# Mixing tokens by constant matrices with Strassen's seven products, on a TensorE-bound kernel

## The chip, the cores and the metric

The kernel runs on one core of a Trainium2 chip. The metric is the device time of one execution, in microseconds (us). A profile of one execution goes with each kernel. Engines in it are PE (TensorE matmul), PEld (TensorE weight load), DVE (VectorE), ACT (ScalarE), POOL (GpSimd) and SP (SyncE, which issues the DMAs). A line number such as L292 is a line of the kernel that was profiled, so the same instruction has another number in another kernel.

## The reference, cut to what matters

There are 32 batches of 512 tokens with 128 features, and one constant 512x512 matrix `adj`. Four layers follow each other, each as `x = x + layer(relu(layernorm(x)))`:

```python
# layer 0: att is a masked softmax made of adj, M the identity
out = einsum('ij,bjg->big', att * M, h @ W[0]) + einsum('ij,bjg->big', att * (1 - M), h @ W[1]) + bias
# layer 1: Chebyshev hops of adj, given twice
x1 = einsum('bnf,nw->bwf', h, A);  x2 = 2 * einsum('bnf,nw->bwf', x1, A) - h
out = relu(concat(h, x1, x2, x1, x2) @ Theta1 + bias)
# layer 2: message passing with adj squared element by element
messages = einsum('nm,bnd->bmd', adj * adj, relu(h @ psi))
out = relu(concat(messages, h) @ phi1) @ phi2 + phi2_b
# layer 3: attention, exp(8 tanh(. / 8)) * adj, normalised
```

In layers 0, 1 and 2 the tokens are mixed by matrices that are the same for every batch: `att` without its diagonal, `adj` and `cheb = 2 adj adj - I`, and `adj * adj`.

## The kernel before

All is float32. Batches go in pairs (16 pairs). A coroutine for each pair and layer emits the work, and a list scheduler in the compiler sets the order in which each engine gets it. The preparation builds `att` and `cheb`; for pairs 0 to 3 it also does the first part of layer 0 (normalising, transposing, the product `p_g` with W[1]). The mixings are these:

```python
def mixed(h, mat, tag, name, copy):          # layers 1 and 2, one batch
    p = bank(f"p_{name}")                    # a PSUM bank
    for t in range(NT):                      # NT = 4 blocks of 128 tokens
        nc.tensor.matmul(p, h[:, t, :], mat[:, t, :], start=(t == 0), stop=(t == NT - 1))
    s = late.tile([P, N], F32, tag=tag, name=name)
    copy(s, p)
    return s

def layer0(q):                               # one pair, both batches side by side
    hT, g = early.pop(q)
    hd = [straight(hT, b, adiag, f"hd_{q}_{b}") for b in range(2)]     # GpSimd
    ...
    for t0 in range(0, NT, 2):
        po = bank(f"p_l0_{q}_{t0}").rearrange("p (t b f) -> p t b f", t=2, b=2)
        for i in range(2):
            for s in range(NT):
                nc.tensor.matmul(po[:, i], attT[:, s, blk(t0 + i)], g[:, s], start=(s == 0), stop=False)
            for b in range(2):
                nc.tensor.matmul(po[:, i, b], hd[b][:, blk(t0 + i)], w0[:, 0, :], start=False, stop=(b == 1))
        nc.vector.tensor_add(xv, po, xv)
```

From pair 4 on the transposed tile is made by VectorE (32x32 blocks) and two DMAs through DRAM: `hb`, `d`, `hT`. All of x is loaded in the first 25 us.

## Time and profile before

The median was 1062.07 us (3 runs, 1061.74 to 1065.86). A layer is timed here from TensorE's first instruction of it to its first of the next, and layer 3 from its first score product (`p_score`), though a few of its projections already stand among the last products of layer 2. The last layer ends with the span.

| stage | before, us | what TensorE does per pair |
|---|---|---|
| preparation | 67.5 | builds att and cheb |
| layer 0 | 172.7 | mixing, diagonal, p_g: 10.48 us where nothing waits |
| layer 1 | 305.5 | two mixings and three projections: 19.10 us |
| layer 2 | 226.8 | p_feat, one mixing, p_phi, p_l: 13.88 us |
| layer 3 | 288.7 | scores, attention |

The lines behind this table, and how they are read, are in the prediction below: TensorE is busy 97% of the span, and the one large hole is at the start of layer 0.

### The profile page before, as it was taken

To read this page: it belongs to the slowest core of one execution; us is meant where nothing else is said; L and a number is where in the kernel's file an instruction comes from. 1 tells how busy PE (TensorE), PEld (TensorE's weight loads), DVE (VectorE), ACT (ScalarE), POOL (GpSimd) and SP (SyncE) were. 2 spreads that over 40 slices of the span, in tenths; PEclk is the share of its full clock that TensorE was granted. 3 is DMA by queue.
4 is the path that set the end of the run, shared out by engine and by line. 5 is a ranking of instruction groups with operands and counts; after the bars stand their busy time and mean duration, and the time that the engine had idled before them with its cause. 6 is when DMAs were issued, how large, how long until landed. Compare 5 with 4: busy or idle time off the path is not lost.

```text
span 1061.2 us, 13502 instructions
## 1 busy us (share of the span) xinstructions
PE 1025.7 (97%) x4966; PEld 698.4 (66%) x4966; DVE 561.5 (53%) x1280; ACT 413.7 (39%) x877; POOL 233.4 (22%) x214
## 2 busy tenths in 40 slices
PE   4996999999999999999989999999999999999997
PEld 3566999995565665655655555555567777777775
DVE  8924666643243342432655787666675444544443
ACT  5722333501132221322756532222275555544443
POOL 3332444322000000000633200000023333333332
PEclk9998999999999999999999999999999999999999
DMA  9525233421112121121434333222212121121111
GB/s 274 128 55 144 80 88 112 133 66 37 44 49 71 40 64 56 42 78 40 139 80 119 116 102 105 77 78 80 79 51 90 53 68 59 61 65 56 50 31 40
DMA packets 82226, 84.91 MB, mean 80 GB/s; under 512 B 7152, under 2 KB 72944, under 8 KB 82160
## 3 DMA queue, kind: packets, MB, share of 16 engines
q1 hardware_dynamic: 82160, 84.05, 27.4%
q8 instruction: 39, 0.64, 0.3%
q14 instruction: 27, 0.22, 0.1%
HBM read 42.08 MB, written 39.85 MB: 77 GB/s over the span
## 4 chain that ended last, share of the span: by engine, by line
PE 89%; SPq 4%; DMA 2%; ACT 2%; issue 2%; DVE 1%; POOL 0%; POOLq 0%; DVEq 0%; ACTq 0%
PE p_msgT L241 11%; PE p_x1T L241 10%; PE p_x2T L241 10%; PE p_l L257 10%; PE p_av L558 10%; PE p_score L546 10%; PE p_l L470 9%; PE p_feat L257 3%; PE p_hv L257 3%; PE p_phi L516 3%; PE p_phi L517 3%; PE p_qkh L534 2%; PE p_g L257 2%; PE p_l L472 2%; SPq L96 2%; SPq L108 2%
## 5 line engine op out<-in xcount | busy, mean ns | idle before, releaser
L200 ACT ACTIVATE h<-x,sh,rs 128x128 f32<-128x128 f32 x384 | 154.2, 482 | 29.2 <-DVE hb_hT L227 15.4
L551 POOL TENSOR_TENSOR ex<-ex,adjTx 128x512 f32<-128x512 f32 x64 | 83.3, 1303 | 333.1 <-ACT ex L549 324.0
L227 DVE STREAM_TRANSPOSE hb_hT<-h 128x512 f32<-128x512 f32 x120 | 82.7, 699 | 103.3 <-ACT h L200 86.4
L558 PEld LDWEIGHTS p_av<-hv,ex 128*128 128x128 f32 x1024 | 118.7, 191 | 11.6 <-issue 6.9
L558 PE MATMUL p_av<-hv,ex 128*128 128x129 f32 x1024 | 121.3, 275 | 2.3 <-POOL ex L551 2.0
L547 ACT ACTIVATE ex<-p_score 128x512 f32<-128x512 f32 x128 | 71.8, 587 | 130.8 <-PE p_score L546 78.7
L470 PE MATMUL p_l<-g,attT 128*128 128x256 f32 x512 | 122.0, 381 | 0.0
L241 PE MATMUL p_msgT<-sq,feat 128*128 128x512 f32 x256 | 114.0, 598 | 3.2 <-ACT feat L508 3.2
L546 PE MATMUL p_score<-qkh,hT 128*128 128x512 f32 x256 | 115.1, 592 | 0.0
L241 PE MATMUL p_x1T<-adj_s,h 128*128 128x512 f32 x256 | 115.1, 592 | 0.0
L241 PE MATMUL p_x2T<-cheb,h 128*128 128x512 f32 x256 | 115.1, 592 | 0.0
L470 PEld LDWEIGHTS p_l<-g,attT 128*128 128x128 f32 x512 | 93.1, 192 | 10.2
L183 DVE BATCH_NORM_STATS2 bn<-x 128x6 f32<-128x256 f32 x256 | 93.3, 415 | 1.8
L241 PEld LDWEIGHTS p_msgT<-sq,feat 128*128 128x128 f32 x256 | 49.1, 192 | 64.9 <-issue 57.8
L241 PEld LDWEIGHTS p_x2T<-cheb,h 128*128 128x128 f32 x256 | 48.6, 190 | 61.2 <-issue 61.0
L186 ACT ACTIVATE sd<-bn,eps 128x8 f32<-128x8 f32 x64 | 18.0, 299 | 176.9 <-DVE bn L183 176.9
L241 PEld LDWEIGHTS p_x1T<-adj_s,h 128*128 128x128 f32 x256 | 47.4, 190 | 53.6 <-issue 53.3
L551 DVE TENSOR_TENSOR ex<-ex,adjTx 128x512 f32<-128x512 f32 x64 | 45.8, 716 | 65.5 <-ACT ex L549 65.5
L243 ACT COPY x2T<-p_x2T 128x512 f32<-128x512 f32 x32 | 18.7, 584 | 152.8 <-PE p_x2T L241 152.7
L549 ACT ACTIVATE ex<-ex 128x512 f32<-128x512 f32 x128 | 76.5, 630 | 1.8
L546 PEld LDWEIGHTS p_score<-qkh,hT 128*128 128x128 f32 x256 | 46.2, 190 | 46.4 <-issue 44.5
L243 DVE COPY x1T<-p_x1T 128x512 f32<-128x512 f32 x32 | 22.1, 691 | 99.8 <-PE p_x1T L241 99.8
(129 smaller groups left out, 1392.6 us busy)
## 6 DMA issues: line engine op xcount, KB each, us to landing
d_hT<-hb_hT SPq DMA_DIRECT2D x240, 128.0 KB, 2.4
hT<-d_hT SPq DMA_DIRECT2D x60, 512.0 KB, 3.3
x<-in_x_dram SPq DMA_DIRECT2D x32, 256.0 KB, 5.5
out_dram<-x SPq DMA_DIRECT2D x32, 256.0 KB, 2.3
adj_s<-in_adj_dram SPq DMA_DIRECT2D x4, 256.0 KB, 3.4
adjTx<-adjT SPq DMA_DIRECT2D x16, 64.0 KB, 2.0
adjx<-adj_s SPq DMA_DIRECT2D x16, 64.0 KB, 2.0
th<-in_L_gnn_Theta_dram SPq DMA_DIRECT2D x1, 320.0 KB, 5.9
```

The source lines that it names most:

```text
L183: nc.vector.bn_stats(st[:, k].rearrange("p e s -> p (e s)"), xt[q][:, b, t : t + 2, :].rearrange("p t f -> p f t"))
L200: nc.scalar.activation(h[:, b, t, :], xt[q][:, b, t, :], AF.Relu, bias=shift[q][:, i : i + 1], scale=scale[q][:, i : i + 1])
L227: nc.vector.transpose(hb[:, :, b].rearrange("p j t r -> p t j r"), h[:, b].rearrange("p t (j c) -> p t j c", c=QR))
L241: nc.tensor.matmul(p, h[:, t, :], mat[:, t, :], start=(t == 0), stop=(t == NT - 1))
L243: copy(s, p)
L257: nc.tensor.matmul(p[:, blk(t)], hT(t), w, start=(i == 0), stop=(i == len(terms) - 1))
L470: nc.tensor.matmul(po[:, i], attT[:, s, blk(t0 + i)], g[:, s], start=(s == 0), stop=False)
L546: nc.tensor.matmul(ps, hT[:, t, b, :], qkh, start=True, stop=True)
L547: nc.scalar.activation(ex[:, t, :], ps, AF.Tanh, scale=1.0 / (8.0 * math.sqrt(D)))
L549: nc.scalar.activation(ex[:, t, :], ex[:, t, :], AF.Exp, scale=8.0)
L551: eng.tensor_mul(ex[:, t, :], ex[:, t, :], adjTx[:, t, :])
L558: nc.tensor.matmul(po[:, i, : D + 1], ex[:, t, blk(i0 + i)], hv[:, t, :], start=(t == 0), stop=(t == NT - 1))
```

## The change

A product of 2x2 block matrices takes eight block products, or seven by Strassen's scheme in Winograd's form, if some blocks are added before and some results after. Here the matrix is constant, so its block sums are formed once. A pair of batches gives the other factor its 2x2 blocks (two halves of tokens by two batches). The intent is to have an eighth fewer TensorE columns in the mixings of layers 0, 1 and 2, with the additions on engines that have time. Memory for this comes from four square tiles in place of five, and from loading the upper half of x during layer 0.

```diff
+    def sum_blocks(mat, name, eng):          # once for a matrix; a21 is overwritten in place
+        eng.tensor_sub(s3, a11, a21)
+        eng.tensor_add(a21, a21, a22)
+        eng.tensor_sub(s2, a21, a11)
+        eng.tensor_sub(s4, a12, s2)
+        return {1: a11, 2: a12, 3: s4, 4: a22, 5: a21, 6: s2, 7: s3}
+    def right_blocks(half, name, engs):      # for each pair: four subtractions, "rt"
+    ORDER = ((1, "a", True), (6, "c", True), (5, "d", True), (7, "c", False), (2, "a", False),
+             (4, "c", False), (3, "d", False))      # product, bank, first into the bank
     ...
+            if k == 1:   nc.scalar.copy(u[:, 0], pv)                # read out a partial sum,
+            elif k == 6: nc.vector.tensor_add(u[:, 1], pv, u[:, 0]) # then more is added to the bank
     ...
+    sums["att"] = sum_blocks(attT, "att", nc.vector)
+    sums["adj"] = sum_blocks(adj_s, "adj", nc.gpsimd)
+    sums["cheb"] = sum_blocks(cheb, "cheb", nc.gpsimd)
     ...
-            nc.vector.tensor_copy(g[:, :, b, :], pg)
+            (nc.scalar.copy if b else nc.vector.tensor_copy)(g[:, :, b, :], pg)
     ...
+    for q in range(NQ // 2, NQ):
+        waiting[q - NQ // 2].append(loads(q))       # x of pair q, eight pairs ahead
```

Layer 0 uses `right_blocks` with VectorE and GpSimd by turns; layers 1 and 2 use GpSimd alone. `sums["sq"]` for layer 2 is formed by GpSimd during layer 1.

More of the change, by code (lines that the diff above doesn't have):

```diff
@@ L66 @@
     const = ctx.enter_context(tc.tile_pool(name="const", bufs=1))
-    xpool = ctx.enter_context(tc.tile_pool(name="xpool", bufs=NQ))
+    xpool = ctx.enter_context(tc.tile_pool(name="xpool", bufs=NQ // 2))
     stats = ctx.enter_context(tc.tile_pool(name="stats", bufs=NQ + 2))
@@ L83, in square_tile @@
     def square_tile(name):
-        return const.tile([P, NT, N], F32, tag="square", name=name, bufs=5)
+        return const.tile([P, NT, N], F32, tag="square", name=name, bufs=4)
     def crossed(ap):
@@ L103 @@
     xt = []
-    for q in range(NQ):
+    for q in range(NQ // 2):
         xt.append(xpool.tile([P, 2, NT, D], F32, tag="x", name=f"x_{q}"))
@@ L136 @@
     kw = load_rows(k_w, "kw")[:, 0, :]
-    for b in range(8, B):
+    for b in range(8, B // 2):
         load_x(b)
@@ L235, in transposed @@
         return hT
-    def mixed(h, mat, tag, name, copy):
-        p = bank(f"p_{name}")
-        for t in range(NT):
-            nc.tensor.matmul(p, h[:, t, :], mat[:, t, :], start=(t == 0), stop=(t == NT - 1))
-        s = late.tile([P, N], F32, tag=tag, name=name)
-        copy(s, p)
-        return s
+    H = N // 2
+    sums = {}
+    def sum_blocks(mat, name, eng):
+        a11, a12 = mat[:, 0:2, 0:H], mat[:, 2:4, 0:H]
+        a21, a22 = mat[:, 0:2, H:N], mat[:, 2:4, H:N]
+        extra = const.tile([P, 3, 2, H], F32, tag="sums", name=f"sums_{name}", bufs=3)
+        s2, s3, s4 = extra[:, 0], extra[:, 1], extra[:, 2]
+        eng.tensor_sub(s3, a11, a21)
[3 more added lines that the diff above has]
+        return {1: a11, 2: a12, 3: s4, 4: a22, 5: a21, 6: s2, 7: s3}
@@ new lines, in right_blocks @@
+    def right_blocks(half, name, engs):
+        t = late.tile([P, 4, 2, D], F32, tag="rt", name=f"rt_{name}", bufs=2)
+        b11, b12, b21, b22 = half(0, 0), half(0, 1), half(1, 0), half(1, 1)
+        engs[0].tensor_sub(t[:, 0], b12, b11)
+        engs[1].tensor_sub(t[:, 1], b22, t[:, 0])
+        engs[2].tensor_sub(t[:, 2], b22, b12)
+        engs[3].tensor_sub(t[:, 3], b21, t[:, 1])
+        return {1: b11, 2: b21, 3: b22, 4: t[:, 3], 5: t[:, 0], 6: t[:, 1], 7: t[:, 2]}
+    ORDER = ((1, "a", True), (6, "c", True), (5, "d", True), (7, "c", False), (2, "a", False),
+             (4, "c", False), (3, "d", False))
@@ new lines, in products, with by_feature @@
+    def products(name, form, left, right, evict):
+        banks = {}
+        for k, g, first in ORDER:
+            if first:
+                banks[g] = bank(f"p_{name}_{g}")
+            form(banks[g], left[k], right[k], first)
+            evict(k, banks[g])
+            yield
+    def by_feature(p, a, b, first):
+        for k in range(2):
+            nc.tensor.matmul(p[:, :H], b[:, k, :], a[:, k, :], start=(first and k == 0),
+                             stop=(k == 1), skip_group_check=True)
@@ new lines, in by_token, with mixed, evict, evict2 @@
+    def by_token(p, a, b, first):
+        for i in range(2):
+            for k in range(2):
+                nc.tensor.matmul(p[:, i * D : (i + 1) * D], a[:, k, blk(i)], b[:, k, :],
+                                 start=(first and i == 0 and k == 0), stop=(k == 1),
+                                 skip_group_check=True)
+    def mixed(name, left, right, dst):
+        m1 = late.tile([P, 3, H], F32, tag="u", name=f"u_{name}", bufs=2)
+        def evict(k, p):
+            p = p[:, :H]
+            if k == 1:
+                nc.scalar.copy(m1[:, 0], p)
+            elif k == 6:
+                nc.vector.tensor_add(m1[:, 1], p, m1[:, 0])
+            elif k == 7:
+                nc.vector.tensor_add(m1[:, 2], p, m1[:, 0])
+            elif k == 5:
+                return
+            elif k == 2:
+                nc.scalar.copy(dst[:, 0, :H], p)
+            elif k == 4:
+                nc.vector.tensor_add(dst[:, 0, H:], p, m1[:, 0])
+            elif k == 3:
+                nc.vector.tensor_add(dst[:, 1, :H], p, m1[:, 1])
+        def evict2(k, p):
+            evict(k, p)
+            if k == 5:
+                held.append(p)
+            if k == 7:
+                nc.vector.tensor_add(dst[:, 1, H:], held[0][:, :H], m1[:, 2])
+        held = []
+        return products(name, by_feature, left, right, evict2)
@@ L259, in projected, with pair_tile @@
         return tiles(p)
+    def pair_tile(name):
+        return work.tile([P, 2 * N + 2 * NT], F32, tag="pair", name=name, bufs=5)[:, : 2 * N]
     early = {}
@@ L270, in layer0_first @@
         yield
-        g = work.tile([P, NT, 2, D], F32, tag="g", name=f"g_{q}", bufs=4)
+        g = pair_tile(f"g_{q}").rearrange("p (t b f) -> p t b f", t=NT, b=2)
         for b in range(2):
             pg = projected(f"p_g_{q}_{b}", (at(hT, b), w0[:, 1, :]))
-            nc.vector.tensor_copy(g[:, :, b, :], pg)
+            (nc.scalar.copy if b else nc.vector.tensor_copy)(g[:, :, b, :], pg)
         early[q] = hT, g
@@ L282, in transpose_square @@
             nc.scalar.copy(dst[:, j, :], p)
-    adjT = square_tile("adjT")
+    adjT = prep.tile([P, NT, N], F32, name="adjT")
     cheb = square_tile("cheb")
@@ L385 @@
                                 ecol[:, kk : kk + 1], OP.is_equal, OP.mult)
-    att = square_tile("att")
+    att = prep.tile([P, NT, N], F32, name="att")
     diag = prep.tile([P, NT, P], F32, name="diag")
@@ L428 @@
     cross_rows(adjTx, adjT)
-    adjx = square_tile("adjx")
-    cross_rows(adjx, adj_s)
+    sums["adj"] = sum_blocks(adj_s, "adj", nc.gpsimd)
+    sums["cheb"] = sum_blocks(cheb, "cheb", nc.gpsimd)
     th12 = const.tile([P, 2, D], F32, name="th12")
@@ L447 @@
     late = ctx.enter_context(tc.tile_pool(name="late", bufs=4))
+    for q in range(NQ // 2, NQ):
+        xt.append(late.tile([P, 2, NT, D], F32, tag="x", name=f"x_{q}", bufs=NQ // 2))
     def straight(hT, b, scale, name):
-        s = late.tile([P, N], F32, tag="hs", name=name, bufs=3)
+        s = late.tile([P, N], F32, tag="hs", name=name, bufs=2)
         src = hT[:, :, b, :].rearrange("p b (a c) -> p a b c", c=QR)
@@ L459, in straight, with loads @@
         return s
+    def loads(q):
+        load_x(2 * q)
+        load_x(2 * q + 1)
+        yield
     def layer0(q):
@@ L464, in layer0, with x_of, diagonal @@
         nc.gpsimd.tensor_add(xt[q], xt[q], b0[:, None, None, :].to_broadcast([P, 2, NT, D]))
+        right = right_blocks(lambda J, b: g[:, 2 * J : 2 * J + 2, b, :], f"g_{q}",
+                             (nc.vector, nc.gpsimd, nc.vector, nc.gpsimd))
         yield
-        for t0 in range(0, NT, 2):
-            po = bank(f"p_l0_{q}_{t0}").rearrange("p (t b f) -> p t b f", t=2, b=2)
+        def x_of(I, b):
+            return xt[q][:, b, 2 * I : 2 * I + 2, :]
+        def diagonal(p, I, b, first):
@@ L468, in layer0 @@
             for i in range(2):
-                for s in range(NT):
-                    nc.tensor.matmul(po[:, i], attT[:, s, blk(t0 + i)], g[:, s], start=(s == 0), stop=False)
-                for b in range(2):
-                    nc.tensor.matmul(po[:, i, b], hd[b][:, blk(t0 + i)], w0[:, 0, :], start=False,
-                                     stop=(b == 1))
-            xv = xt[q][:, :, t0 : t0 + 2, :].rearrange("p b t f -> p t b f")
-            nc.vector.tensor_add(xv, po, xv)
+                nc.tensor.matmul(p[:, i * D : (i + 1) * D], hd[b][:, blk(2 * I + i)], w0[:, 0, :],
+                                 start=(first and i == 0), stop=True, skip_group_check=True)
@@ new lines, in layer0, with evict @@
+        u = late.tile([P, 3, 2, D], F32, tag="u", name=f"u_l0_{q}", bufs=2)
+        held = {}
+        def evict(k, p):
+            pv = p[:, :H].rearrange("p (i f) -> p i f", i=2)
+            if k == 1:
+                nc.scalar.copy(u[:, 0], pv)
+                nc.gpsimd.tensor_add(x_of(1, 0), x_of(1, 0), u[:, 0])
+            elif k == 6:
+                nc.vector.tensor_add(u[:, 1], pv, u[:, 0])
+                nc.gpsimd.tensor_add(x_of(0, 1), x_of(0, 1), u[:, 1])
+            elif k == 5:
+                held["d"] = pv
+            elif k == 7:
+                nc.vector.tensor_add(u[:, 2], pv, u[:, 0])
+                nc.vector.tensor_add(u[:, 2], held["d"], u[:, 2])
+                nc.gpsimd.tensor_add(x_of(1, 1), x_of(1, 1), u[:, 2])
+            elif k == 2:
+                diagonal(p, 0, 0, False)
+                nc.vector.tensor_add(x_of(0, 0), pv, x_of(0, 0))
+            elif k == 4:
+                diagonal(p, 1, 0, False)
+                nc.vector.tensor_add(x_of(1, 0), pv, x_of(1, 0))
+            elif k == 3:
+                diagonal(p, 0, 1, False)
+                nc.vector.tensor_add(x_of(0, 1), pv, x_of(0, 1))
@@ L476, in layer0 @@
+        for _ in products(f"l0_{q}", by_token, sums["att"], right, evict):
+            pass
+        p = bank(f"p_l0_{q}_e")
+        diagonal(p, 1, 1, True)
+        nc.vector.tensor_add(x_of(1, 1), p[:, :H].rearrange("p (i f) -> p i f", i=2), x_of(1, 1))
         ln_stats(q)
@@ L481, in layer1 @@
         hT = transposed(h, f"hT1_{q}")
+        right = right_blocks(lambda J, b: h[:, b, 2 * J : 2 * J + 2, :], f"h_{q}", [nc.gpsimd] * 4)
         yield
-        x1T, x2T, hs = [], [], []
-        for b in range(2):
-            x1T.append(mixed(h[:, b], adj_s, "mT", f"x1T_{q}_{b}", nc.vector.tensor_copy))
-            x2T.append(mixed(h[:, b], cheb, "x2T", f"x2T_{q}_{b}", nc.scalar.copy))
-            hs.append(straight(hT, b, None, f"hs_{q}_{b}"))
+        x1T = pair_tile(f"x1T_{q}").rearrange("p (b w) -> p b w", b=2)
+        x2T = pair_tile(f"x2T_{q}").rearrange("p (b w) -> p b w", b=2)
+        mixes = (mixed(f"x1T_{q}", sums["adj"], right, x1T), mixed(f"x2T_{q}", sums["cheb"], right, x2T))
+        for _ in zip(*mixes):
+            pass
+        hs = [straight(hT, b, None, f"hs_{q}_{b}") for b in range(2)]
         yield
         for b in range(2):
-            po = projected(f"p_l1_{q}_{b}", (columns(hs[b]), th[:, 0, :]), (columns(x1T[b]), th12[:, 0, :]),
-                           (columns(x2T[b]), th12[:, 1, :]))
-            y = late.tile([P, NT, D], F32, tag="y", name=f"y1_{q}_{b}", bufs=3)
+            po = projected(f"p_l1_{q}_{b}", (columns(hs[b]), th[:, 0, :]), (columns(x1T[:, b]), th12[:, 0, :]),
+                           (columns(x2T[:, b]), th12[:, 1, :]))
+            y = late.tile([P, NT, D], F32, tag="y", name=f"y1_{q}_{b}", bufs=2)
             nc.vector.tensor_add(y, po, spread(b1, NT))
@@ L505, in layer2 @@
             pf = projected(f"p_feat_{q}_{b}", (at(hT, b), psi))
-            feat.append(late.tile([P, NT, D], F32, tag="y", name=f"feat_{q}_{b}", bufs=3))
+            feat.append(late.tile([P, NT, D], F32, tag="y", name=f"feat_{q}_{b}", bufs=2))
             nc.vector.tensor_add(feat[b], pf, spread(psib, NT))
@@ L509, in layer2 @@
         yield
-        msgT = [mixed(feat[b], sq[0], "mT", f"msgT_{q}_{b}", nc.vector.tensor_copy) for b in range(2)]
+        right = right_blocks(lambda J, b: feat[b][:, 2 * J : 2 * J + 2, :], f"feat_{q}", [nc.gpsimd] * 4)
+        msgT = pair_tile(f"msgT_{q}").rearrange("p (b w) -> p b w", b=2)
+        for _ in mixed(f"msgT_{q}", sums["sq"], right, msgT):
+            pass
         nc.gpsimd.tensor_add(xt[q], xt[q], phi2b[:, None, None, :].to_broadcast([P, 2, NT, D]))
         yield
-        h1T = []
+        h1T = pair_tile(f"h1T_{q}").rearrange("p (b w) -> p b w", b=2)
         for b in range(2):
@@ L516, in layer2 @@
             nc.tensor.matmul(ph, phi1[:, 1, :], hT[:, :, b, :], start=True, stop=False)
-            nc.tensor.matmul(ph, phi1[:, 0, :], msgT[b], start=False, stop=True)
-            h1T.append(late.tile([P, N], F32, tag="x2T", name=f"h1T_{q}_{b}"))
-            nc.scalar.activation(crossed(h1T[b]), split(ph), AF.Relu, bias=phi1b)
+            nc.tensor.matmul(ph, phi1[:, 0, :], msgT[:, b], start=False, stop=True)
+            nc.scalar.activation(crossed(h1T[:, b]), split(ph), AF.Relu, bias=phi1b)
         yield
         for b in range(2):
-            po = projected(f"p_l2_{q}_{b}", (columns(h1T[b]), phi2))
+            po = projected(f"p_l2_{q}_{b}", (columns(h1T[:, b]), phi2))
             nc.vector.tensor_add(xt[q][:, b], po, xt[q][:, b])
@@ L534, in layer3 @@
             nc.tensor.matmul(pp, qk, hT[:, :, b, :], start=True, stop=True)
-            qkh = late.tile([P, N], F32, tag="mT", name=f"qkh_{q}_{b}")
+            both = work.tile([P, 2 * N + 2 * NT], F32, tag="pair", name=f"qkh_hv_{q}_{b}", bufs=5)
+            qkh = both[:, :N]
             nc.vector.tensor_copy(crossed(qkh), split(pp))
             pv = projected(f"p_hv_{q}_{b}", (at(hT, b), vw))
-            hv = late.tile([P, NT, D + 1], F32, tag="hv", name=f"hv_{q}_{b}", bufs=3)
+            hv = both[:, N : N + NT * (D + 1)].rearrange("p (t f) -> p t f", f=D + 1)
             nc.gpsimd.memset(hv[:, :, D : D + 1], 1.0)
@@ L565, in layer3 @@
             nc.sync.dma_start(out[2 * q + b].rearrange("(t p) f -> p t f", p=P), xt[q][:, b])
-    sq = []
     def square():
-        sq.append(square_tile("sq"))
+        sq = square_tile("sq")
+        for a in range(NT):
+            for b in range(NQR):
+                nc.sync.dma_start(sq[a * QR : (a + 1) * QR, b, :],
+                                  adj[a * P + b * QR : a * P + (b + 1) * QR, :])
+        yield
         for i in range(NT):
-            nc.gpsimd.tensor_mul(split(sq[0][:, i, :]), crossed(adjx[:, i, :]), crossed(adjx[:, i, :]))
+            s = late.tile([P, N], F32, tag="hs", name=f"sq_{i}", bufs=2)
+            nc.gpsimd.tensor_mul(split(s), crossed(sq[:, i, :]), crossed(sq[:, i, :]))
+            nc.gpsimd.tensor_copy(sq[:, i, :], s)
+        sums["sq"] = sum_blocks(sq, "sq", nc.gpsimd)
         yield
     waiting = [[layer0(q)] for q in range(NQ)]
+    for q in range(NQ // 2, NQ):
+        waiting[q - NQ // 2].append(loads(q))
     for q in range(EARLY, NQ):
```

## The prediction

> **What bounds the kernel now.** I read the page's head first, then the stretches by stage, the chain in order of time, and the timeline of TensorE where the chain leaves it. The page:
>
> ```profile
> PE 1025.7 (97%) x4966; PEld 698.4 (66%) x4966; DVE 561.5 (53%) x1280; ACT 413.7 (39%) x877; POOL 233.4 (22%) x214
> ...
> PE 89%; SPq 4%; DMA 2%; ACT 2%; issue 2%; DVE 1%; POOL 0%; POOLq 0%; DVEq 0%; ACTq 0%
> ```
>
> TensorE is the bound, and carries 89% of the chain that ended last. By stage (start, up to the end of layer 0, layer 1, layer 2, layer 3; columns: us, then busy us of PE, PEld, DVE, ACT, POOL, then clock, DMA share, GB/s):
>
> ```profile
> 95.00:240.00 145.00, 145.00 (x862) 133.18 (x862) 85.40 (x209) 43.52 (x118) 53.05 (x35) 0.98 0.33 97
> 240.00:545.00 305.00, 305.00 (x1278) 182.55 (x1277) 118.33 (x227) 90.32 (x221) 41.79 (x43) 1.00 0.22 63
> 545.00:780.00 235.00, 231.70 (x935) 135.78 (x933) 159.64 (x368) 92.30 (x179) 21.07 (x11) 0.99 0.31 90
> 780.00:1061.00 281.00, 274.80 (x1570) 199.96 (x1570) 137.97 (x334) 138.78 (x254) 84.88 (x92) 1.00 0.18 57
> ```
>
> From 95 us on TensorE has nearly no gap, so fewer TensorE passes shorten the kernel one for one, as long as no other engine holds it up. The chain gives the price of a pass:
>
> ```profile
> 233.85 1.73 PE p_l L470 x8
> ...
> 240.37 3.44 PE p_x1T L241 x8
> 243.80 3.43 PE p_x2T L241 x8
> ...
> 254.10 5.36 PE p_l L257 x48
> ```
>
> The program writes 256 matmuls for p_x1T and p_x2T together; the page counts 512, so each float32 matmul is two passes. A pass of 512 columns takes 3.43/8 = 0.429 us, of 256 columns 1.73/8 = 0.216, of 128 columns 5.36/48 = 0.112. The one large hole lies at the start of layer 0:
>
> ```profile
> 85.39 0.61 PE L472 MATMUL p_l<-w,hd 128*128 128x128 f32 x4
> 94.40 3.78 PE L257 MATMUL p_g<-w,hT 128*128 128x128 f32 x16 [8.40 <-DMA hT<-d_hT]
> 97.97 2.77 PE L470 MATMUL p_l<-g,attT 128*128 128x256 f32 x8
> ```
>
> The wait of 8.40 us is for the transposed tile of pair 4. Its transfer stands behind 32 row-crossing DMAs that the sync queue issues at about 0.63 us each from 65.3 us. After it, starts lie 3.57 and 2.60 us apart, where 1.79 and 1.73 are normal: 2.65 us more.
>
> **What the Trainium skill says.** "TensorE: Matmul & The Clock Gate", Back-to-back issue gap: the gap grows with the columns streamed plus a small constant. The three prices agree (0.429, 0.216, 0.112), so splitting a pass is nearly free. Same page, Part 1: TensorE idle for about 3.4 us falls to half clock and needs about as long to recover; the slow p_g above fits. "SBUF — State Buffer", Who interferes with whom: a VectorE instruction with two SBUF inputs and a GpSimd one that reads SBUF exclude each other for a whole instruction. It agrees: a scale-and-shift instruction, 0.15 us elsewhere, took 2.09 us from 16.64, while GpSimd's add ran from 15.75 to 18.71. "PSUM — Partial Sum Buffer", PSUM bank collisions: two engines may not touch one bank together, so accesses are guarded by bank; a product added to a bank must wait until the former partial sum has been read out. No trace of before shows such a wait in the middle of a sum.
>
> **The change part by part.**
> 1. Layer 1, per pair of batches. Before: two mixings of 16 passes of 512 columns, 2 x 6.87 us, and 48 passes of 128, 5.36: 19.10 us, which the chain shows as its period. After: seven products of 4 passes of 256 columns, 28 x 0.216 = 6.05 per mixing; period 17.46. Saved: 1.64 x 16 = 26 us. The new work lies beside: VectorE gets ten adds of 128x256 (0.46 us each as an estimate, between 0.346 us for 128x128 and 0.692 for 128x512 of its rows) in place of two copies, some 9 us in all of 17.5; GpSimd gets four subtractions of about 0.73 us (0.774 is one of that size) beside two copies, 4.2 of 17.5. The two mixings alternate, so a partial sum has three other products, 2.6 us, to be read out. I expect no wait, and charge 1 us for the squaring of adj on GpSimd, which falls in here.
> 2. Layer 2, per pair. Before 6.87 + 1.79 + 1.79 + 3.43 = 13.88 us (the chain: 13.87). After 13.06; at most 0.82 x 16 = 13 us saved. Here one mixing runs alone: between product 6 and product 7 into the same bank lies a single product, 0.86 us, and in that time VectorE must see the matmul end (0.2 after its last slot: a pass's record is 0.17 longer than its slot, and a copy of p_g began 0.03 after the record's end), add (0.46) and signal (0.1; a p_g began 0.06 after the copy it waited for). That fits only if VectorE is free. It is 68% busy, and the compiled order puts layer 3's normalising pieces of 0.34 us between these adds. I charge 0.25 us a pair, 4 us, and 2 us more at the first pair, where the right operands come through GpSimd. Net 7 us.
> 3. Layer 0, per pair. Before 32 x 0.216 + 16 x 0.112 + 16 x 0.112 (p_g) = 10.48. After 56 x 0.112 + 3.58 = 9.85; saved 0.65 where nothing waits. But VectorE's list in that time (nine adds, eight statistics at 0.35, two transposes at 0.62, a copy, small ones) is 8.5 us, and GpSimd's (two products 2.5, a bias add 2.35, five of 0.73) also 8.5: both over 85%, and excluding each other on the subtractions. I charge 0.45 us a pair. Over 14 pairs, 3 us are left.
> 4. Start of layer 0. Half of the crossing DMAs leave this place and adjTx has its own square, so its 16 DMAs go early; x's upper half waits for the preparation's memory, but pair 4's transfer follows soon after. The 8.40 + 2.65 = 11 us disappear. In their place: in the compiled order GpSimd does, after its last cheb instruction (ended at 64.7 in the trace), eight block sums of 128x512 (1.25 us each: 10), with four VectorE sums excluding them (2.5), then two hd products (2.5), and only then the subtraction (0.73) that product 6 of pair 0 needs. That is 80.4 us; TensorE is done with product 1 at about 68.8. A wait of 11.6 us, and 2.7 of slow clock. Net, with the 0.7 us wait for hd gone: 2 to 3 us worse.
> 5. Layer 3 is the same matmuls in the same order. Its exponentials get three squares instead of four. One lives some 11.5 us (scores 3.4, last tanh, four exp, a GpSimd product: 8; then 3.6 of use) at a need of one per 8.77 us: two would nearly do. 0.
> 6. Loading half of x later takes 4 MB out of the first 25 us, which are not bound by it; they move to where DMA is a third busy. 0 to 1 us gained.
>
> Sum: 26 - 1 + 7 + 3 - 2.5 + 0.5 = 33 us; 1062 - 33 = 1029.
>
> **The rivals.**
> A: VectorE or GpSimd becomes the bound of layer 0. For it: the two lists of 8.5 us, the exclusion, and that a late sum holds TensorE through the bank. Against: the right operands are prepared a pair ahead, GpSimd has its slack late in the period, ACT's copy of product 1 stands ahead of its normalising. If it holds, a pair takes 11.5 us instead of 10.3: 17 us more, 1046.
> B: The PSUM waits eat layer 2 too, and show in layer 1: 0.8 us a pair in layer 2, 0.5 in layer 1. For it: 0.86 us of room against 0.76. Against: layer 1's room of 2.6. Then 1029 + 9 + 8 = 1046; with A, 1063, no gain.
> C: All hidden, the start wait as well: 26 + 13 + 9 + 8 = 56 us, 1006. Against: GpSimd's queue at the start keeps its order, and that is the most certain of the waits.
>
> **Range and chances.** The 26 us of layer 1 rest on measured prices and wide room; alone they come to 1036, still over 2% (limit 1040.8). The rest is small terms of both signs, each uncertain by 5 to 10 us; A is the most likely to hurt. Low 1013 is most of C without the start, high 1049 is A or B alone and some. Faster by over 2%: 0.75; within: 0.22; slower: 0.03, which would need A and B together and more.
>
> **What would show it.** Passes of p_x1T of 256 columns 0.216 us apart and a layer 1 period of 17.5 us: step 1. In layer 2 a period of 13.1 to 13.5, with TensorE's waits on VectorE at the second product into a bank: step 2. A layer 0 period near 10.3 with VectorE over 85% busy: step 3. A TensorE wait of 10 to 13 us near 69, put down to GpSimd's subtraction: step 4. p_av's wait as small as before (2.3 us): step 5. The prediction is wrong if the short passes cost over 0.22 us because of their weight loads, if layer 0's period exceeds 11, or if GpSimd's work delays layer 1.

## The result, and the profile after

The changed kernel took 1033.34 us (median of 4 runs, 1032.86 to 1033.77), beside 1063.71 for the kernel before on the same chip. The ratio is 0.9714, with a 95% interval of 0.969 to 0.9738.

The page's busy shares and chain, after:

```profile
PE 983.9 (95%) x5926; PEld 814.3 (79%) x5926; DVE 654.9 (64%) x1556; ACT 443.7 (43%) x973; POOL 400.6 (39%) x438
...
PE 85%; DVE 8%; ACT 3%; DMA 1%; SPq 1%; issue 1%; POOL 0%; POOLq 0%; DVEq 0%; ACTq 0%
```

TensorE has 42 us less work and more instructions. GpSimd's work has grown from 233 to 401 us. DVE has gone from 1% of the chain to 8%: TensorE now waits for evictions at some places. The stretches by stage, cut at the new borders (us, then busy us of PE, PEld, DVE, ACT, POOL, then clock, DMA share, GB/s):

```profile
95.00:240.00 145.00, 140.34 (x1226) 139.10 (x1225) 118.14 (x315) 58.88 (x158) 116.81 (x116) 0.99 0.39 105
240.00:520.00 280.00, 278.21 (x1660) 254.97 (x1659) 165.27 (x353) 96.72 (x254) 89.99 (x108) 1.00 0.26 71
520.00:748.00 228.00, 222.41 (x1120) 171.38 (x1118) 170.69 (x416) 102.23 (x211) 65.89 (x77) 0.99 0.33 93
748.00:1031.00 283.00, 276.50 (x1571) 201.59 (x1570) 138.22 (x334) 138.99 (x254) 83.49 (x93) 0.99 0.19 57
```

In layer 0 (first line) VectorE and GpSimd are busy 118 and 117 of 145 us, where they had 85 and 53.

| stage | before | after | difference |
|---|---|---|---|
| preparation | 67.5 | 66.4 | -1.1 |
| layer 0 | 172.7 | 172.4 | -0.3 |
| layer 1 | 305.5 | 281.2 | -24.3 |
| layer 2 | 226.8 | 220.7 | -6.1 |
| layer 3 | 288.7 | 290.4 | +1.7 |
| span | 1061.2 | 1031.1 | -30.1 |

The first row is no effect that can be relied on. In the profiles of the kernels below the preparation took from 65.6 to 70.7 us, though its work differs little or not at all. So I compare layers, not whole times, where a difference is under 5 us.

**Layer 1** came out as the chain shows it (start, us, what):

```profile
251.06 5.36 PE p_l L338 x48
256.42 0.87 PE p_x1T_a L285 x4
...
268.51 5.36 PE p_l L338 x48
```

Product 1 of p_x2T begins at 257.29, so four passes of 256 columns take 0.87 us, 0.217 each, and one period is 268.51 - 251.06 = 17.45 us.

**Layer 0** gained next to nothing. Here is TensorE's timeline at its start (start, us, instruction, and in brackets the idle time before it and what ended it):

```profile
66.38 1.06 PE L292 MATMUL p_l_a<-g,attT 128*128 128x128 f32 x8
68.02 0.71 PE L292 MATMUL p_l_a<-g,attT 128*128 128x128 f32 x4 [0.58 <-ACT u_l L574]
79.12 2.07 PE L292 MATMUL p_l_c<-rt_g,sums_att 128*128 128x128 f32 x8 [10.39 <-DMA d_hT<-hb_hT]
...
84.40 0.63 PE L292 MATMUL p_l_a<-g,attT 128*128 128x128 f32 x4
...
110.32 2.46 PE L338 MATMUL p_g<-w,hT 128*128 128x128 f32 x16 [2.51 <-DMA hT<-d_hT]
```

TensorE does product 1 of pair 0 and half of product 2, and then waits 10.39 us before product 6. The profile names a DMA as the releaser. That DMA has nothing to do with product 6; the instruction reads `rt_g`, and GpSimd's queue shows when that came:

```profile
63.59 1.27 POOL L253 TENSOR_TENSOR sums_adj<-adj_s 128x512 f32<-128x512 f32 x1
...
74.31 1.44 POOL L256 TENSOR_TENSOR sums_cheb<-cheb,sums_cheb 128x512 f32<-128x512 f32 x1
75.72 2.66 POOL L544 TENSOR_TENSOR hd<-hT,adiag 128x512 f32<-128x512 f32 x2
78.34 0.72 POOL L264 TENSOR_TENSOR rt_g<-g,rt_g 128x256 f32<-128x256 f32 x1
```

The eight block sums of adj and cheb ran without a break from 63.59 to 75.7 us, then the two products with the diagonal, then the subtraction, which ended at 79.06. Product 6 began 0.06 later. After the wait three products took 84.40 - 79.12 = 5.28 us where 3 x 0.89 is normal: 2.6 us of slow clock (the trace has a granted clock of 0.5 there, until 84.44). At 110.32 follows a wait that I had not foreseen, for the transposed tile of pair 5: 2.51 us and, from the starts behind it (112.56, 114.27 and 115.59, 3.03 us for two products of 0.89, and 2.24 for a p_g of 1.79), 1.7 us of slow clock.

In between the steady period is short. From 122 us on, p_g starts lie 9.83 us apart, and TensorE is busy all of the 70 us from 125 to 195. So the passes saved what they should, and the waits took it. With 1.79 us for a p_g that the preparation does for four pairs, layer 0 without waits would be 16 x 10.48 - 7.2 = 160.5 us before and 16 x 9.85 - 7.2 = 150.4 after. It lost 12.2 us to waits and slow clock before, and 22.0 after.

**Layer 2**, one pair, the mixing only:

```profile
662.11 1.03 PE L285 MATMUL p_msgT_c<-sums_sq,rt_feat 128*128 128x256 f32 x4
662.97 1.03 PE L285 MATMUL p_msgT_d<-sq,rt_feat 128*128 128x256 f32 x4
663.83 0.59 PE L285 MATMUL p_msgT_a<-sq,feat 128*128 128x256 f32 x2
664.26 1.07 PE L285 MATMUL p_msgT_c<-sums_sq,rt_feat 128*128 128x256 f32 x4
665.17 0.60 PE L285 MATMUL p_msgT_a<-sq,feat 128*128 128x256 f32 x2
665.60 0.38 PE L338 MATMUL p_feat<-psi,hT 128*128 128x128 f32 x2
665.94 1.10 PE L285 MATMUL p_msgT_c<-sq,rt_feat 128*128 128x256 f32 x4
```

Between the products 6, 7 and 4 into bank c stand one product and a half (0.86 + 0.43 us) and then only half a product and two passes of p_feat (0.43 + 0.22 us). The starts from 664.26 to 665.17 lie 0.91 us apart where 0.86 is normal, and the two passes of p_feat from 665.60 to 665.94 take 0.34 for 0.22. The second of these gaps is VectorE's: its add to product 7's partial sum ended at 665.79, and product 4 began 0.15 later. Such gaps are too short to be listed as waits, but a pair of the steady stretch takes 13.28 us where the passes alone make 13.06. Two longer waits for the same adds are listed early in the layer, 1.28 us at 583.91 and 0.25 at 597.48; at the first of them ACT's copy of product 1 and VectorE's add stood behind normalising pieces.

The 6.1 us are good to about 1 us. In the twelve kernels with Strassen's products layer 2 took 219.5 to 219.8 us where the clock was at half for 3.41 us after the layer's first wait, and 220.4 to 221.0, the changed kernel among them, where it was for 6.83 us.

**Layer 3**: nearly all of the 1.7 us is one line, the last passes of the kernel; first the kernel before, then after:

```profile
1054.44 2.50 PE L558 MATMUL p_av<-hv,ex 128*128 128x129 f32 x20 [0.42 <-POOL ex L551]
```

```profile
1022.60 4.14 PE L687 MATMUL p_av<-qkh_hv,ex 128*128 128x129 f32 x20 [0.42 <-POOL ex L680]
```

The same wait stands before both, but the mean granted clock was 1.00 over these passes before (1054.4 to 1057.0 us) and 0.58 after (1022.6 to 1026.7). Over the fourteen profiles the line has 2.50 or 4.14 us and nothing else, and layer 3 has 288.7 to 288.8 or 290.3 to 290.4 us with it. Of the twelve kernels with Strassen's products, whose layer 3 is the same code, four have the shorter line and eight the longer, so I take it for an accident of the execution. But each kernel was profiled once: that one kernel has both is not shown.

### The profile page after: what moved, and what is told of

Its sections match the earlier page's. It is cut to its first block, busy times and chain, and to the rows that moved or that the text cites. A ratio compares the mean times of both kernels' runs of the same rounds, so it can differ in the third digit from the quotient of the medians.

```text
span 1031.1 us, 16161 instructions
## 1 busy us (share of the span) xinstructions
PE 983.9 (95%) x5926; PEld 814.3 (79%) x5926; DVE 654.9 (64%) x1556; ACT 443.7 (43%) x973; POOL 400.6 (39%) x438
## 4 chain that ended last, share of the span: by engine, by line
PE 85%; DVE 8%; ACT 3%; DMA 1%; SPq 1%; issue 1%; POOL 0%; POOLq 0%; DVEq 0%; ACTq 0%
PE p_av L687 11%; PE p_score L675 10%; PE p_l L338 10%; PE p_msgT_c L285 4%; PE p_x1T_c L285 4%; PE p_x2T_c L285 4%; PE p_l_c L292 4%; PE p_hv L338 3%; PE p_msgT_a L285 3%; PE p_x1T_a L285 3%; PE p_x2T_d L285 3%; PE p_x2T_a L285 3%; PE p_x1T_d L285 3%; PE p_qkh L662 3%; PE p_msgT_d L285 2%; PE p_feat L338 2%
## 5 line engine op out<-in xcount | busy, mean ns | idle before, releaser
L687 PEld LDWEIGHTS p_av<-qkh_hv,ex 128*128 128x128 f32 x1024 | 120.3, 193 | 11.6 <-issue 6.9
L687 PE MATMUL p_av<-qkh_hv,ex 128*128 128x129 f32 x1024 | 122.9, 277 | 2.2 <-POOL ex L680 1.4
L675 PE MATMUL p_score<-qkh_hv,hT 128*128 128x512 f32 x256 | 115.2, 592 | 0.0
L680 DVE TENSOR_TENSOR ex<-ex,adjTx 128x512 f32<-128x512 f32 x64 | 45.9, 717 | 75.7 <-ACT ex L678 75.7
L675 PEld LDWEIGHTS p_score<-qkh_hv,hT 128*128 128x128 f32 x256 | 46.3, 190 | 46.4 <-issue 44.5
L263 POOL TENSOR_TENSOR rt_h<-h 128x256 f32<-128x256 f32 x16 | 11.6, 726 | 133.2 <-PE p_x2T_c L285 132.1
L263 POOL TENSOR_TENSOR rt_feat<-feat,feat 128x256 f32<-128x256 f32 x16 | 11.6, 728 | 126.3 <-ACT feat L634 126.3
L555 POOL TENSOR_TENSOR x<-x,b 128x1024 f32<-128x1024 f32 x16 | 37.8, 2365 | 40.4 <-ACT h L204 25.9
L640 POOL TENSOR_TENSOR x<-x,phi2b 128x1024 f32<-128x1024 f32 x16 | 38.0, 2374 | 33.1 <-ACT h L204 33.1
L338 PE MATMUL p_l<-th,x1T 128*128 128x128 f32 x256 | 49.5, 275 | 0.0
L338 PE MATMUL p_l<-th,x2T 128*128 128x128 f32 x256 | 49.5, 275 | 0.0
L338 PE MATMUL p_l<-th,hs 128*128 128x128 f32 x256 | 49.5, 275 | 0.0
L292 PE MATMUL p_l_c<-rt_g,sums_att 128*128 128x128 f32 x256 | 36.7, 290 | 12.7 <-DMA d_hT<-hb_hT 10.4
```

Source lines behind the costliest of these rows:

```text
L292: nc.tensor.matmul(p[:, i * D : (i + 1) * D], a[:, k, blk(i)], b[:, k, :], start=(first and i == 0 and k == 0), stop=(k == 1), skip_group_ ...
L338: nc.tensor.matmul(p[:, blk(t)], hT(t), w, start=(i == 0), stop=(i == len(terms) - 1))
L640: nc.gpsimd.tensor_add(xt[q], xt[q], phi2b[:, None, None, :].to_broadcast([P, 2, NT, D]))
L675: nc.tensor.matmul(ps, hT[:, t, b, :], qkh, start=True, stop=True)
L680: eng.tensor_mul(ex[:, t, :], ex[:, t, :], adjTx[:, t, :])
L687: nc.tensor.matmul(po[:, i, : D + 1], ex[:, t, blk(i0 + i)], hv[:, t, :], start=(t == 0), stop=(t == NT - 1))
```

## The experiments

Twelve kernels ran, all correct. The table has layer 0 and TensorE's waits in it; layer 1 was 281.2 us in every kernel with Strassen's products. Waits of 0.15 us or less, which the profile doesn't list, are left out.

| kernel | time, us (ratio to before) | layer 0 | wait for first right operand | for pair 5's tile | for u_l (VectorE), sum |
|---|---|---|---|---|---|
| before | 1062.07 | 172.7 | none (0.7 for hd) | 8.4 (pair 4's) | none |
| after | 1033.34 (0.9714) | 172.4 | 10.4 | 2.5 | 2.3 |
| plain_all | 1063.45 (1.0019) | 173.6 | none (1.8 for hd) | 4.8 | none |
| x_later | 1034.96 (0.9735) | 172.2 | 10.4 | 2.6 | 2.3 |
| late_cheb | 1030.51 (0.9695) | 168.6 | 5.1 | 2.4 | 4.1 |
| late_both | 1029.18 (0.9679) | 167.3 | 1.9 | 2.5 | 6.7 |
| late_both_v | 1026.76 (0.9657) | 165.8 | 1.9 | 2.4 | 5.5 |
| first_early | 1029.31 (0.969) | 169.4 | 1.9 | none | 9.2 |
| tail | 1026.31 (0.9667) | 165.1 | 1.9 | 2.5 | 5.4 |
| tail_fe | 1029.35 (0.9695) | 164.6 | 1.9 | none (0.5 for pair 15's) | 8.8 |
| after_act | 1037.67 (0.9769) | 174.8 | 10.4 | 2.7 | 3.8 |
| tail_act | 1030.81 (0.9701) | 170.2 | 1.9 | 2.7 | 7.4 |
| halves | 1027.35 (0.9657) | 166.2 | 1.9 | 2.6 | 4.1 |
| halves_rf | 1027.38 (0.9654) | 165.6 | 1.2 | 2.6 | 4.1 |

My theory was that the gain is the passes saved, and that layer 0's gain was lost to GpSimd's queue at its start. The rivals: the late loads of x, or the memory freed by the preparation, hold the start; the gain comes from moved work, not from the products; VectorE and GpSimd bound layer 0.

### Moving the block sums: late_cheb, late_both, late_both_v

A first try only moved the calls down in the program. It was compiled and not run: I saw the sums at the same place as before, hoisted by the scheduler because they were ready. So each sum is tied, in issue order only, behind an instruction of its engine in a given pair:

```diff
-    sums["cheb"] = sum_blocks(cheb, "cheb", nc.gpsimd)
+    def late_sums(mat, name, eng, marks):       # the four lines of sum_blocks, each as
+        with tc.issue_after(marks[-1].ins):     # marks: the engine's last x-add of each pair
+            eng.tensor_sub(s3, a11, a21)
+        yield
+    waiting[5].append(late_sums(cheb, "cheb", nc.gpsimd, marks))
```

late_cheb moves cheb's sums, late_both adj's too, late_both_v does both on VectorE.

> Theory (GpSimd's queue): the four block sums of cheb leave the start of layer 0, where they took 1.5 us each beside VectorE's sums, and run one per pair behind pairs 4 to 7. That shortens the queue ahead of the first right operand by about 6 us: the first wait falls from 10.4 us to 4 to 5 us, and the time from 1033 to 1025 to 1028. Rival (the loads of x's upper half, or the memory freed by the preparation, hold the start): the wait stays at 10 us and the time at 1033, plus up to 2 us because GpSimd has one more instruction in four pairs.

> Theory: all eight block sums of adj and cheb leave the start and run one per pair behind pairs 4 to 11. The wait of 10.4 us in front of product 6 of pair 0 falls under 2 us and most of its slow clock (2.6 us) goes with it; the second wait (2.5 us for pair 5's transposed tile, and 2.1 of slow clock) is a consequence of the first and goes too: 1016 to 1020. Rival for the second wait (the transposed tile's transfers stand behind x's loads in SyncE's queue): TensorE arrives earlier and waits there longer, 5 to 12 us, so that the time is 1022 to 1030. Rival for the first: no change, 1033. If GpSimd's load bounds layer 0, the period of 9.83 us rises by 0.5 to 1.3 in the eight pairs that carry a sum: 4 to 10 us back.

> As late_both, but VectorE does the eight sums, at some 0.7 us each instead of 1.3. Theory: both engines have over 1 us left in a pair of 9.83 us, so the same time within 2 us of late_both, 1016 to 1020. Rival (one of the two lists bounds layer 0): the two differ by 4 us or more, and the one whose engine is the bound shows a longer period in pairs 4 to 11.

Measured: the first wait went 10.4, 5.1, 1.9 us with eight, four and no sums in the queue, so GpSimd's queue is the cause. The time from the start of layer 0 to pair 5's p_g went from 43.9 us (110.3 - 66.4) to 37.8 and 33.8, the full 10 us. GpSimd's queue in late_both:

```profile
69.48 3.07 POOL L563 TENSOR_TENSOR hd<-hT,adiag 128x512 f32<-128x512 f32 x2 [3.04 <-PE p_qk L545]
72.51 0.90 POOL L285 TENSOR_TENSOR rt_g<-g,rt_g 128x256 f32<-128x256 f32 x1
```

Now GpSimd itself stands idle for 3.04 us, until TensorE's last product of the preparation. The likely reason is that the tiles `hd` and `rt` lie in the memory that the preparation gives back; no run tests it.

Two expectations failed. The second wait did not go with the first: it stayed at 2.4 to 2.5 us in all three. And layer 0 fell only by 3.8, 5.1 and 6.6 us. From pair 5's p_g to the end of layer 0, after took 128.5 us, late_both 133.5, late_both_v 132.1. So 5 and 3.6 us were given back in the pairs that carry a sum, where TensorE waits for an eviction, as in late_both:

```profile
151.02 1.16 PE L313 MATMUL p_l_c<-rt_g,sums_att 128*128 128x128 f32 x8 [1.28 <-DVE u_l L596]
```

### The loads of x two pairs later: x_later

```diff
-        waiting[q - NQ // 2].append(loads(q))
+        waiting[q - NQ // 2 + 2].append(loads(q))
```

> Each pair of x's upper half is loaded two pairs later, and nothing else changes. Theory (GpSimd's queue): the first wait stays at 10.4 us; the second (pair 5's tile, 2.5 us and 2.1 of slow clock) goes only if the loads stood ahead of its transfers, so 1029 to 1034. Rival (the loads hold the start of layer 0): the first wait falls by 5 us or more, 1020 to 1027.

Measured: layer 0 in 172.2 us, the first wait 10.39 us again, the second 2.58. The loads hold neither. (The whole time, 1034.96, is within the range that preparations of other length give.)

### All mixings plain again: plain_all

```diff
-        mixes = (mixed(f"x1T_{q}", sums["adj"], right, x1T), mixed(f"x2T_{q}", sums["cheb"], right, x2T))
+        plain(f"x1T_{q}", adj_s, lambda b: h[:, b], x1T)      # four matmuls of 512 columns a batch
+        plain(f"x2T_{q}", cheb, lambda b: h[:, b], x2T)       # and so in layers 0 and 2
-    sums["adj"] = sum_blocks(adj_s, "adj", nc.gpsimd)
+    unread_sums(adj_s, "adj", nc.gpsimd)                      # the same sums, written elsewhere
```

> The changed kernel with its loads, squares and block sums of adj and cheb left as they are (the sums are computed and not read), but every mixing by plain products again. Theory (the gain is the passes saved): layer 1 goes back from 281.2 to 305.4 us, layer 2 from 220.7 to 226.8, and layer 0 from 172.4 to about 181, since its period goes from 9.83 to 10.48 us and the wait behind GpSimd's sums stays, now for the product with the diagonal: 1066 to 1073 us, slower than the kernel before. Rival (the later loads and the fewer squares earn a good part): layer 0 or layer 1 keeps some of the gain and the time is 1050 or less.

Measured: layer 1 in 305.5 us, as before the change, and layer 2 in 225.4. (The 1.4 us between this and 226.8 are clock: after the same first wait, 3.2 us, the granted clock was 0.50 for 3.4 us in the profile of before, and 1.00 in this one.) The kernel is level with the one before (1.0019, interval 1.0002 to 1.0036). So the loads, the squares and the rest of the change earn nothing, and the products all. In layer 0 my number was wrong: 173.6 us, not 181. Two reasons can be read in its trace. The unread sums don't overwrite adj, so the scheduler did adj's earlier, and three sums, not eight, stood in the queue. And a plain pair needs nothing from GpSimd until its diagonal; TensorE had 4 x 1.73 us of products to do first:

```profile
67.69 7.07 PE L579 MATMUL p_l<-g,attT 128*128 128x256 f32 x32
74.60 0.61 PE L581 MATMUL p_l<-w,hd 128*128 128x128 f32 x4
```

There is no wait in front of this diagonal; the 1.8 us in the table stand before the next pair's. Strassen's order asks for GpSimd's operand in its second product. No run separates the two reasons. As an estimate, behind the changed kernel's queue, whose `hd` ended at 78.38, 12.0 us after the start of layer 0, this diagonal, due after 6.9 us, would have waited some 5 us: the longer queue alone makes a wait, and Strassen's order makes it longer.

### The second wait: first_early, after_act

The chain to pair 5's tile, read off all engines in late_both:

```profile
82.25 0.37 ACT L593 COPY u_l<-p_l_a 128x256 f32<-128x256 f32 x1 [11.48 <-PE p_l_a L313]
...
85.34 3.19 ACT L204 ACTIVATE h<-x,sh,rs 128x128 f32<-128x128 f32 x8 [0.91 <-DVE sh L194]
...
87.08 0.70 DVE L231 STREAM_TRANSPOSE hb_hT<-h 128x512 f32<-128x512 f32 x1
...
92.89 0.70 DVE L231 STREAM_TRANSPOSE hb_hT<-h 128x512 f32<-128x512 f32 x1
...
98.82 0.34 SPq L238 DMA_DIRECT2D hT<-d_hT  x1
...
102.96 2.39 PE L359 MATMUL p_g<-w,hT 128*128 128x128 f32 x11 [2.46 <-DMA hT<-d_hT]
```

The Trainium skill, "PSUM — Partial Sum Buffer", Engine vs sequencer instructions, states that the queues of ScalarE, VectorE and GpSimd are strict FIFO. The trace agrees: ACT stood 11.48 us in front of the copy of pair 1's first product, with pair 5's normalising behind it, and VectorE did the second transposition 4.4 us after ACT was done (88.53), behind statistics and adds. first_early (late_both_v with this chain begun one pair earlier) and after_act (the changed kernel with both p_g copies on ACT) attack it from two sides:

```diff
-        waiting[q - EARLY].append(layer0_first(q))
+        waiting[max(0, q - EARLY - 1)].append(layer0_first(q))
```

```diff
-            (nc.scalar.copy if b else nc.vector.tensor_copy)(g[:, :, b, :], pg)
+            nc.scalar.copy(g[:, :, b, :], pg)
```

> late_both_v with the first part of layer 0 (statistics, normalising, transposed tile, p_g) begun one pair earlier from pair 5 on. Theory (the second wait is a fixed chain: ACT normalises pair 5 only after the copy of pair 1's first product, VectorE transposes its second half 4 us after ACT is done, then 9 us of transfers; TensorE has less than that to do): the wait of 2.4 us on pair 5's tile and 1.5 us of slow clock go, layer 0 falls from 165.8 to 161 to 163 us, and the time to 1022 to 1025. Rival (SyncE's queue or the transfers are the limit): the wait stays, 1026 to 1028.

> The changed kernel with one edit: ACT copies both p_g of a pair, where VectorE had one of them; in layer 0 that takes 0.67 us a pair from VectorE (8.3 of 9.83) and gives ACT 0.58 (it is half busy). Theory (pair 5's tile is late because VectorE, at its limit in pairs 0 to 4, does the second transposition 4 us after ACT is done, part of it waiting for p_g itself): the first wait stays at 10.4 us, the second falls from 2.5 to under 1 us and its 2.1 us of slow clock goes, and the small waits on u_l shrink; layer 0 falls from 172.4 to 167 to 170 us. Rival (the wait is the transfers' own time): the second wait stays at 2.5 us and layer 0 at 172.

Measured: first_early removed the wait for the tile, so it is the chain's start that is late and not the transfers that limit. But layer 0 rose to 169.4 us: TensorE waited 9.2 us for evictions in place of 5.5, two of them 1.3 and 2.3 us with slow clock behind. Starting work earlier put it in front of evictions: before the wait of 2.3 us ACT did eight normalising pieces (96.92 to 100.11) and a copy of p_g ahead of its copy of product 1 (100.48), and VectorE two transpositions and a copy of p_g ahead of its add (101.35).

after_act was worse than the changed kernel, 174.8 us in layer 0, and the wait for the tile stayed at 2.67. So 0.67 us a pair less for VectorE did not bring the tile earlier, and my theory that VectorE's load makes it late is not borne out; ACT got more to do by the same edit, so it is not excluded either. What happened in a steady pair instead:

```profile
157.04 0.88 ACT L204 ACTIVATE h<-x,sh,rs 128x128 f32<-128x128 f32 x2 [0.69 <-DVE sh L194]
157.82 0.35 ACT L574 COPY u_l<-p_l_a 128x256 f32<-128x256 f32 x1
158.20 0.42 DVE L577 TENSOR_TENSOR u_l<-p_l_c,u_l 128x256 f32<-128x256 f32 x1 [1.20 <-ACT u_l L574]
158.68 1.16 PE L292 MATMUL p_l_c<-rt_g,sums_att 128*128 128x128 f32 x8 [0.28 <-DVE u_l L577]
```

With the copies moved, the scheduler put two normalising pieces ahead of ACT's copy of product 1, and that copy stands on a path: product 1, ACT's copy, VectorE's add to product 6, TensorE's product 7 into the same bank. A pair took 10.37 us instead of 9.83, with less work on VectorE. In this kernel the same wait of 10.39 us was put down to GpSimd's `rt_g` by the profile, and not to a DMA.

### Sums placed elsewhere: tail, tail_fe, tail_act, halves, halves_rf

tail does four of adj's sums on VectorE while TensorE forms cheb, and the other five behind late pairs; tail_fe and tail_act add the two edits above.

```diff
+    with tc.issue_after(last_own.ins):           # VectorE's last step of att, near 48 us
+        three(); one(s4); two(s4); four()        # adj's sums, a21 + a22 formed in s4 for a time
+    waiting[12].append(later(three_c, one_c, two_c, four_c))     # cheb's, behind pairs 11 to 14
+    waiting[14].append(later(adj_one))                           # a21 + a22 in its place
```

> late_both_v with the eight sums placed otherwise: four of adj's in VectorE's idle stretch while TensorE forms cheb (48 to 62 us; one is formed in a second place because adj is still read there), the other five behind pairs 11 to 14, where no pair's first part is left to do. Theory (in pairs 4 to 11 a sum doesn't fit beside the 8.3 us that VectorE and GpSimd each have in 9.83): the 3 to 5 us given back there return, layer 0 falls from 165.8 to 161 to 163 us. Rival (something else in those pairs): layer 0 stays at 165 to 167 us.

> tail and first_early together. If the two losses are separate, as the theory has it, they add: layer 0 at 157 to 160 us and a time of 1019 to 1022. If they are one loss seen twice, layer 0 is as in the better of the two.

> The same edit on tail. Theory: the waits on u_l in the pairs that carry sums (3.7 us in pairs 11 to 14) and pair 5's wait (2.5, with 1.6 of slow clock) shrink by half or more: layer 0 from 165.1 to 159 to 162 us, 1020 to 1023. Rival (ACT's copy of product 1 comes late now, behind two copies and the normalising): new waits on ACT, layer 0 stays at 164 to 167 us.

Measured: layer 0 in 165.1, 164.6 and 170.2 us, none as low as expected. The time lost in pairs 4 to 11 was won back (no wait is listed between 108.7 and 197.9 us), but 3.7 us of waits for u_l stand in the last pairs. Of these 1.3 us are not due to the sums: the changed kernel, which has none there, has waits of 0.49 and 0.80 at the same places. tail_fe was better than tail in layer 0 by only 0.5 us, so the two gains don't add: the 2.5 us at pair 5's tile went, and the first three waits for u_l grew from 0.6, 0.2 and 0.6 us to 1.8, 0.8 and 2.3. tail_act was worse for the reason found in after_act; its rival was right. VectorE's queue in tail shows two of the sums:

```profile
205.00 1.57 DVE L270 TENSOR_TENSOR cheb<-cheb 128x512 f32<-128x512 f32 x1
...
207.45 0.68 DVE L271 TENSOR_TENSOR sums_cheb<-cheb 128x512 f32<-128x512 f32 x1
```

The same kind of sum took 0.68 us where it met only the end of a GpSimd instruction, and 1.57 where GpSimd's product was running (from 204.76 to 206.02). halves therefore does one more of cheb's sums early and cuts the last four in two each, behind pairs 4 to 11, and halves_rf has GpSimd make pair 0's right operands before its diagonal products:

```diff
+        for half in (slice(0, 1), slice(1, 2)):
+            with tc.issue_after(marks[-1].ins):
+                run(k, half)
```

```diff
+        if not q:
+            with tc.issue_after(last_rt[-1].ins):
+                hd = spread_hd()
```

> As tail, but one more sum (of cheb) is done in VectorE's idle stretch, and the four that remain are cut in halves of 128x256, one half behind each of pairs 4 to 11. Theory (a sum costs TensorE time only where it is longer than VectorE's gap of about 0.8 us in front of the eviction of product 6): a half takes 0.4 us and fits, the waits on u_l that the sums caused (3.7 us in tail) go, and layer 0 falls from 165.1 to 161 to 163 us: 1022 to 1025. Rival (VectorE's total work counts, not the piece's length, or GpSimd's exclusion doubles each half): layer 0 at 164 to 166 us, as in tail.

> halves with one more order set: for pair 0 GpSimd forms the right operands before its two products with the diagonal. Theory (the 1.9 us that are left of the first wait are those two products, 2.5 us, standing ahead of the operand): the wait falls to under 0.5 us and TensorE may wait up to 0.6 us for the diagonal later, so layer 0 is 1 to 2 us shorter than in halves, 159 to 162 us, and the time 1021 to 1024. Rival (the operand waits for VectorE's first subtraction anyway, or the gain turns into a longer wait for pair 5's tile): layer 0 as in halves, the wait of 2.5 us on the tile grown by what was gained.

Measured: 166.2 and 165.6 us in layer 0; the rival was right. Here is a half in VectorE's queue:

```profile
168.11 1.11 DVE L278 TENSOR_TENSOR sums_cheb<-cheb,sums_cheb 128x256 f32<-128x256 f32 x1
```

A half took 0.41 us at 139.53 and 0.9 to 1.1 at six of the eight places, where GpSimd's product of 1.27 us runs at the same time. So cutting did not help: what VectorE pays at that place is mostly the rest of GpSimd's instruction, not its own length. halves differs from tail in the place of the sums too; late_both_v, with eight whole sums in the same pairs, had layer 0 in 165.8 us. In halves_rf the first wait fell from 1.9 to 1.2 us, not under 0.5, and the slow clock behind it stayed.

late_both_v, tail, halves and halves_rf all beat both kernels. late_both_v is at 0.9657 (0.9642 to 0.9673), halves_rf at 0.9654 (0.9635 to 0.9673), each about 0.6% under the changed kernel's 0.9714 (0.969 to 0.9738); they are not told apart from each other. What keeps layer 0 at 165 us, 15 over its passes, is not settled: no placement that I tried got under 164.6.

## Why the prediction was right or wrong

The time was predicted as 1029 with a range of 1013 to 1049, and was 1033.34. The sum was near, and in it:

- **Step 1, layer 1** (26, less 1): right. 24.3 us were gained, the price of a pass is 0.216 to 0.217 and the period 17.45. The charge of 1 us for the squaring of adj came in by another way: the squares and their sums ran from 340.6 to 354 us and cost the period nothing, while one wait of 1.8 us for `u_x1T` stands at 490.20, after a VectorE add that took 2.29 us beside a GpSimd add of 2.35. plain_all shows that the products alone make the step.
- **Step 2, layer 2** (7 net): right in the sum, 6.1, which its clock leaves open by 1 us. The cost per pair was charged at 0.25 and is 0.22 in the steady stretch (13.28 - 13.06), by the mechanism named, a product that waits for a partial sum to be read, though more of it lies at the third product into the bank than at the second. The first pair's wait was 3.5 us beside 3.2 before, with 0.5 for `u_msgT`. The 1.28 and 0.25 us for VectorE's adds further on were not foreseen.
- **Step 3, layer 0's pairs** (0.45 us a pair given back): wrong. The steady period was 9.83 us, not 10.3, with VectorE and GpSimd busy 85% each (66 us of the 78 from 122 to 200). The engines kept up, so the steady part gained its whole 0.65 us a pair (10.48 - 9.83; the prediction's 0.65 is 0.63 by its own two sums). Two other things took the place of this charge: the wait for pair 5's tile with its slow clock, 4.2 us, and 2.3 us for evictions. The prediction took pair 4's tile, rightly, as no longer late, and did not ask about the next one. That these 6.5 us come so near the 6.3 charged (14 x 0.45) is luck. That the steady pair has nothing to spare, as step 3 feared, is nevertheless what the experiments met: 1.3 us more for GpSimd in a pair cost TensorE up to 1.3 us.
- **Step 4, the start** (2 to 3 us worse): right in cause and near in size. The wait was 10.39 us where 11.6 were worked out; the slow clock 2.6 where 2.7; the start lost 1.2 us net (10.39 + 2.6 against 8.40 + 2.65 + 0.73). late_cheb and late_both show the cause. Steps 3 and 4 together were to gain 0.5 us, and layer 0 gained 0.3, partly by the wrong way.
- **Step 5, layer 3** (0): right. The 1.7 us are the slow clock of the last twenty passes, found in some of the profiles and not in others.
- **Step 6** (0 to 1 gained): not shown. The 1.1 us lie inside the preparation's own variation, and x_later and plain_all show no effect of the loads.

Of the rivals, A (layer 0 bound by the other engines) did not happen in the changed kernel. B did not happen in layer 1 and happened in layer 2 at a quarter of its size. C failed at the start wait, as foretold.

## What to carry to other kernels

Fewer passes shorten a TensorE-bound kernel by passes times price only where every new operand and every eviction is ready in time; before using such a scheme, ask which engine delivers the operand of its second product, and what stands ahead of it in that engine's queue. One-time work for a later stage must not be queued ahead of the first stage's operands, and writing it later in the program is not enough where a scheduler hoists it. Where an engine takes its queue in order, is some 85% busy and is held up by another (VectorE's sums took 0.7 us, or up to 1.7 beside GpSimd), moved work costs what it delays behind it, so measure a placement and don't count its microseconds.

## What the Trainium skill lacked or had wrong

- "SBUF — State Buffer", Who interferes with whom, has the exclusion of VectorE and GpSimd, and that the order of issue decides who waits, but no measure of it for two adders side by side. Here a VectorE sum of 128x512 took 0.67 to 0.69 us alone or when it began first, and 1.0 to 1.7 when a GpSimd instruction was already running and not just ending; one of 128x256 took 0.41 and up to 1.1, and GpSimd's sums went from 1.27 to 1.71: halving the VectorE instruction did not halve its cost.
- "TensorE: Matmul & The Clock Gate", Part 1: The HAM clock gate, gives a free-running window of about 3.4 us, and the half clock after a whole idle window. Shorter waits were also followed by a slow clock here: 2.5 us (after), and 1.94 us in halves, where eight passes then took 2.08 us, while the same 1.94 us in late_both was followed by 1.16. The granted clock stayed at 1.00 in late_both and was 0.50 from 73.31 to 76.72 in halves. The recovery from the long wait covered 5.3 us. It would help to say that a single wait under the window may or may not cost.
- No page has the cost of products that add to a bank whose partial sum is read out in between: with 1.3 and 0.65 us of other work in the room, layer 2 lost 0.22 us a steady pair in gaps too short for a list of waits; with 2.6 us in layer 1 the period of 17.45 had no loss.
